# An attention-plus-FFN kernel on one core: inner passes row by row, a later divide, an earlier value projection and a later last norm

## The chip, the cores and the metric

The kernel runs on one NeuronCore of a Trainium2 chip. The metric is the device time of one execution in microseconds. Before the change the median of three runs is 858.41 us (858.38 to 859.41).

## The reference

The input x has 32 sequences of 256 tokens with 128 features. One layer of post-norm transformer is computed in float32:

```python
# attention: 16 heads of 8; scores get -(i - j) as a decay, and are causal
Q, K, V = (split_heads(x @ W.T + b) for W, b in ((Wq, bq), (Wk, bk), (Wv, bv)))
attn = softmax(where(j > i, -inf, Q @ K.T / sqrt(8)) - (i - j))
x = layernorm(x + (attn @ V) @ Wo.T + bo)
# FFN: every matrix is ternary times a power of two, with a scale per output
h = silu((x @ w1.T) * s1) * ((x @ w2.T) * s2)      # 128 -> 512
h = gelu((h @ h1.T) * sh1)                         # 512 -> 512
h = gelu((h @ h2.T) * sh2)                         # 512 -> 512
x = layernorm(x + (h @ w3.T) * s3)                 # 512 -> 128
```

## The kernel before

**Tiles and steps.** Sequences are handled in 16 pairs of 512 tokens. A step n of the function `step` has two stages. In the attention stage the scores of pair n are weighed (`weigh`) while the score maxima of pair n+1 are taken (`row_maxima`), in 12 iterations. In the feed stage the FFN of pair n-1 runs (`feed`), and the end of pair n's attention (`rest`) is woven between its parts. Nothing is planned by costs or due times: each engine works through its instructions in the order in which the program issues them, and that order is written out by hand with generators. A `yield` ends a piece; whoever holds the generator calls `next` where the following piece shall be issued. (The profile puts nearly every instruction on L56, because a helper there records them, so the tiles' names tell them apart.)

**Exact float32 out of two parts.** The FFN's activations are split into a rounded high part and a low part (`hi`, `lo`, the two slices of `h`, `hodd`, `heven`); each product with a weight block is two matmuls, one for each part. (The kernel tests at run time that the weights lose nothing in the rounded format, and takes this branch if so; the other branch isn't run here.) So each inner layer (h1 into `podd`, h2 into `peven`) has 4 output blocks o times 4 input blocks k times 2 parts, 32 matmuls of 128x512. Blocks o = 0 and 1 are accumulated together in one two-bank PSUM tile, then o = 2, then o = 3. In the first of these passes (line 586 on) the order before is: for o = 0 the blocks k = 0, 1, 2, for o = 1 the same, and then k = 3 for both. The gates write `h` block by block: ScalarE takes the silu (`sg`), VectorE multiplies (`h0w`), rounds it into the high part and subtracts for the low part; the low parts of blocks 0 and 1 are subtracted on GpSimd (line 576).

**What is woven in.** `feed` yields after each of its 4 gates, and ahead of each of the 8 outputs of the inner layers, 12 times in all. At each yield the next piece of `rest` is issued. Before the change those pieces are, in a step in the middle:

1. first half of the last `outputs` (`pa`);
2. its second half, and the copy `oT`;
3. the transposes `pt` and, on VectorE, the divide (`rec`, then `on` twice);
4. `maxima_to_rows` of pair n+1: transposes `pm`, high part `mhi` on ScalarE, low part `mlo` on VectorE, four DMAs on SP;
5. `finish`, first part: transposes `pon`, copy `onT`;
6. `project_values` of pair n+2: matmuls `pv`, four additions `vaug`;
7. `finish`, second part: matmuls `po`, residual addition into x;
8. `first_norm`, statistics `sta`, `mva`, `rsa` and a power on GpSimd (line 275);
9. its normalisation (`x<-x,mva,rsa`).

**The end of a pair.** `last` (pair n-2, in the attention stage of step n) has four pieces: the w3 matmuls `pw<-heven` with the scaling copy `yT`; transposes `py` and the residual `y`; the statistics `stf`, `mvf`, `rsf` with the power on GpSimd; and the normalisation `z` with the store of the result on SP's queue. They are issued in iterations 0, 2, 4 and 6. The heven that the first piece reads comes from the feed stage that has just ended.

**PSUM.** Six of the eight banks are three two-bank tiles (`two`) for scores, gates and inner layers; two banks (`work`) serve everything else, `pt`, `pm`, `pon`, `pv` and `po` among it, so each of those waits until the tile that held its bank has been read.

Of the kernel before, what the change touches and what calls it, by code (L numbers as in the profile page):

```python
# [17 lines left out]
P = 128  # L18
# [21 lines left out]
KC = HID // P  # L40
NPAIR = B // 2
# [18 lines left out]
def tile_attn_ffn(  # L60
# [24 lines left out]
    pe, vec, act, sp = (InOrder(tc, e) for e in (nc.tensor, nc.vector, nc.scalar, nc.sync))  # L85
# [24 lines left out]
    ks = [const.tile([P, W, TOK], F32R, name=f"ks{i}") for i in range(2)]  # L110
# [355 lines left out]
    def outputs(n, a):  # L466
        v = pairs[n]["v"]
        *first, second = pairs[n][("e", a)]
        r, e = divmod(a, 2)
        if e == 0:  # L470
            pairs[n]["pa"] = work(f"pa_{n}_{r}").rearrange("c (b i) -> c b i", b=2)
        pa = pairs[n]["pa"]
        for jc in range(2):
            for b in range(2):
                for c in range(C):
                    h, p = c // 2, c % 2
                    at = VSLOT * (C * r + c) + VHEAD * e
                    pe.matmul(
                        pa[32 * c : 32 * (c + 1), b, jc * P :],
                        lhsT=v[:, 2 * b + jc, at : at + 32],  # L480
                        rhs=second[:, p, h, b, :] if jc else first[h][:, p, b, :],
                        start=(e == b == jc == 0), stop=(e == b == jc == 1),
                        tile_position=(0, 32 * c),
                    )
            if jc == 0:
                yield
        if e == 0:
            return
        oT = op.tile([P, TOK], F32, name=f"oT_{n}_{r}", tag="oT", bufs=1)
        act.copy(oT, pa.rearrange("c b i -> c (b i)"))  # L490
        yield

        if r == 0:
            pairs[n]["on"] = op.tile([P, NT, D], F32, name=f"on_{n}", tag="on", bufs=1)
        on = pairs[n]["on"].rearrange("i t (r e c d) -> i t r e c d", r=2, e=2, c=C)
        po = work(f"pt_{n}_{r}").rearrange("i (t c k) -> i t c k", t=NT, c=C)
        for t in range(NT):
            pe.transpose(po[:, t].rearrange("i c k -> i (c k)"), oT[:, t * P : (t + 1) * P], ident)
        rec = mp.tile([P, NT, C, 2], F32, name=f"rec_{n}_{r}", tag="rec")
        vec.reciprocal(rec, po[:, :, :, HD : HD + VHEAD + 1 : VHEAD])  # L500
        for e in range(2):
            vec.tensor_tensor(
                on[:, :, r, e], po[:, :, :, VHEAD * e : VHEAD * e + HD],
                rec[:, :, :, e : e + 1].to_broadcast([P, NT, C, HD]), ALU.mult,
            )
# [40 lines left out]
    def product(ps, w, parts, start, stop):  # L546

        for i, part in enumerate(parts):
            pe.matmul(
                ps, lhsT=w, rhs=part, start=start and i == 0,  # L550
                stop=stop and i == len(parts) - 1,
            )

    def feed(n, exact, ws, hp, gp):

        final = n == NPAIR - 1
        even, odd = ("odd", "even") if final else ("even", "odd")
        x1T = pairs[n]["x1T"]
        parts = range(2 if exact else 1)
        kind = F32R if exact else F32  # L560
        h = hp.tile([P, len(parts), KC, TOK], kind, name=f"h0_{n}", tag=even)
        for o in range(KC):
            cols = slice(o * P, (o + 1) * P)
            pab = two(f"pw_{n}_{o}")
            pa, pb = pab[:, 0, :], pab[:, 1, :]
            product(pa, ws["w1"][:, 0, cols], [x1T[:, i, :] for i in parts], True, True)
            product(pb, ws["w2"][:, 0, cols], [x1T[:, i, :] for i in parts], True, True)
            sg = gp.tile([P, TOK], F32, name=f"sg_{n}_{o}", tag="sg")
            act.activation(sg, pa, AF.Silu, scale=sc["s1"][:, o : o + 1])
            whole = gp.tile([P, TOK], F32, name=f"h0w_{n}_{o}", tag="whole") if exact else h[:, 0, o, :]  # L570
            vec.scalar_tensor_tensor(
                whole, pb, sc["s2"][:, o : o + 1], sg, ALU.mult, ALU.mult
            )
            if exact:
                vec.tensor_copy(h[:, 0, o, :], whole)
                (nc.gpsimd if o < (1 if final else 2) else vec).tensor_tensor(  # L576
                    h[:, 1, o, :], whole, h[:, 0, o, :].bitcast(F32), ALU.subtract
                )
            yield
        prepare(AF.Gelu)  # L580
        for w, s, nm, tag in (
            (ws["h1"], sc["sh1"], "odd", odd), (ws["h2"], sc["sh2"], "even", even)
        ):
            got = hp.tile([P, len(parts), KC, TOK], kind, name=f"h{nm}_{n}", tag=tag)

            for os in ((0, 1), (2,), (3,)):
                both = two(f"p{nm}_{n}_{os[0]}")
                ph = {o: both[:, o - os[0], :] for o in os}
                for ks in ((0, 1, 2), (3,)):
                    for o in os:  # L590
                        for k in ks:
                            product(
                                ph[o], w[:, k, o * P : (o + 1) * P],
                                [h[:, i, k, :] for i in parts], k == 0, k == KC - 1,
                            )
                for o in os:
                    yield
                    if not exact:
                        act.activation(got[:, 0, o, :], ph[o], AF.Gelu, scale=s[:, o : o + 1])
                        continue  # L600
                    whole = gp.tile([P, TOK], F32, name=f"{nm}w_{n}_{o}", tag="whole")
                    hi, lo = (got[:, i, o, :] for i in range(2))
                    hasty = nm == "even" and o == KC - 1
                    if not hasty:
                        act.activation(hi, ph[o], AF.Gelu, scale=s[:, o : o + 1])
                    act.activation(whole, ph[o], AF.Gelu, scale=s[:, o : o + 1])
                    if hasty:
                        vec.tensor_copy(hi, whole)
                    vec.tensor_tensor(lo, whole, hi.bitcast(F32), ALU.subtract)
            h = got  # L610
        if n < NPAIR - 2:
            prepare(AF.Exp)
        elif not final:
            prepare(AF.Silu)
        pairs[n]["h"] = h
# [47 lines left out]
    def run(gen):  # L663
        for _ in gen:
            pass
# [25 lines left out]
    def step(n, exact=None, ws=None, hp=None, gp=None):  # L691


        side = iter(())
        settling = (
            last(n - 2, exact, ws, gp) if n > 1 else first_norm(0) if n else inexact_weights()
        )
        ahead = project(n + 2) if n + 2 < NPAIR else iter(())
        for i in range(3 * G):
            weigh(n, i)  # L700
            j = i if n else i + LEAD
            if n + 1 < NPAIR and j < 3 * G:
                row_maxima(n + 1, j)
            next(side, None)
            if n and i == 9:
                turn(n - 1, exact)
            if i in (0, 2, 4, 6) if n else i:
                next(settling, None)

            if i in ((3, 4, 5) if n == 1 else (1, 3, 5)):  # L710
                next(ahead, None)
            if i % 3 == 2:
                run(side)
                side = outputs(n, i // 3)
        run(settling)
        run(ahead)
        if n + 2 < NPAIR:
            stack(n + 2, "q")
            stack(n + 2, "k")


        def rest():
            yield from side
            yield
            if n + 1 < NPAIR:
                maxima_to_rows(n + 1)
                yield
            last_steps = finish(n)
            next(last_steps)
            yield  # L730
            if n + 2 < NPAIR:
                project_values(n + 2)
                yield
            yield from last_steps
            if n:
                yield
                yield from first_norm(n)
            if n == NPAIR - 1:
                yield
                turn(n, exact)  # L740

        if n:
            prepare(AF.Silu)
        due = rest()
        for _ in feed(n - 1, exact, ws, hp, gp) if n else ():
            next(due, None)
        run(due)
# [83 lines left out]
```

## Time and profile before

| what | value |
|---|---|
| median of 3 runs | 858.41 us |
| profiled execution, its own time | 859.17 us |
| its span | 857.4 us |
| PE busy | 799.5 us (93%) |
| weight loads (PEld) busy | 561.5 us (65%) |
| VectorE (DVE) busy | 635.0 us (74%) |
| ScalarE (ACT) busy | 519.5 us (61%) |
| GpSimd (POOL) busy | 270.9 us (32%) |
| one step in the middle (428.02 to 476.88) | 48.86 us, PE busy 48.02 |
| its attention stage (435.40 to 459.36) | 23.96 us, PE busy 23.37, DVE busy 21.11 |
| its gates and first inner layer (459.36 to 476.88) | 17.52 us, PE busy 17.27, DVE busy 13.50 |
| the next second inner layer (476.88 to 484.30) | 7.42 us, PE busy 7.42, DVE busy 3.83 |

The middle steps are equal: the second inner layers start 48.86 us apart from 134.87 to 721.18. The last three stretches of that kind are shorter (46.92, 45.68 and 43.62 us). Matmuls are pipelined, so a PE that is busy may still have started late: of two matmuls in a row, the distance of their starts tells more than their durations.

### The profile page before, as it was taken

Reading aid. Unit: us, or ns where it says so; the run is one execution under the profiler, and the core shown is the slowest. Engines: PE = TensorE matmul, PEld = TensorE weight load, DVE = VectorE, ACT = ScalarE, POOL = GpSimd, SP = SyncE. Lnnn points to the kernel's source line nnn. Section 1 sums busy time; section 2 is a strip of 40 time slices with the busy share of each in tenths; the row PEclk is TensorE's granted clock in tenths of the full one; section 3 lists DMA queues with packets and bytes.
Section 4 is the critical chain, followed back from the end, with each engine's and each line's share of the span. In section 5 each row is a group of like instructions: output and inputs, shape, how many; then the busy total and the mean of one; then the engine's idle time right before and its main releaser. Section 6 shows DMA issues by size and latency. Waiting matters only on the chain.

```text
span 857.4 us, 17396 instructions
## 1 busy us (share of the span) xinstructions
PE 799.5 (93%) x7042; PEld 561.5 (65%) x7042; DVE 635.0 (74%) x1231; ACT 519.5 (61%) x713; POOL 270.9 (32%) x354
## 2 busy tenths in 40 slices
PE   4588999999999999999999999999999999999895
PEld 2355667676766767676766767676676767666673
DVE  3677677878778686878778787878778687874664
ACT  1026367666576676657676666657666666658462
POOL 9123332414232241414233240524224141424200
PEclk9558699999999999999999999999999999999998
DMA  6543240220405041140404032040504013000001
GB/s 142 128 147 86 45 101 16 61 67 14 102 14 114 14 101 26 38 90 14 103 13 112 16 74 54 14 102 14 115 13 111 5 48 68 14 5 13 1 1 29
DMA packets 40627, 48.16 MB, mean 56 GB/s; under 512 B 4376, under 2 KB 22040, under 8 KB 40536
## 3 DMA queue, kind: packets, MB, share of 16 engines
q1 hardware_dynamic: 38240, 44.13, 21.8%
q10 hardware_dynamic: 2296, 2.82, 1.4%
q8 instruction: 57, 0.93, 0.5%
q14 instruction: 34, 0.28, 0.1%
HBM read 7.48 MB, written 4.19 MB: 14 GB/s over the span
## 4 chain that ended last, share of the span: by engine, by line
PE 63%; DVE 24%; ACT 5%; issue 3%; DMA 2%; POOL 2%; ACTq 0%; DVEq 0%; POOLq 0%
PE peven L56 13%; PE s L56 9%; PE podd L56 9%; DVE m L56 9%; PE pw L56 8%; PE pa L56 8%; DVE h L56 5%; DVE h0w L56 3%; PE s_0d L56 2%; DVE z L56 2%; PE s_3d L56 2%; PE po L56 2%; PE pq L56 2%; PE pv L56 2%; ACT sg L56 1%
## 5 line engine op out<-in xcount | busy, mean ns | idle before, releaser
L459 POOL TENSOR_SCALAR_AFFINE_SELECT e<-e 128x512 f32<-128x512 f32 x128 | 82.5, 644 | 275.2 <-ACT e L56 275.2
L56 DVE TENSOR_REDUCE m<-s 128x4 f32<-128x1024 f32 x128 | 155.5, 1218 | 16.3 <-PE s L56 16.1
L56 ACT ACTIVATE e<-s 128x1024 f32<-128x1024 f32 x128 | 130.9, 1022 | 55.8 <-PE s L56 26.9
L56 PE MATMUL podd<-h,h_near 128*128 128x512 f32 x512 | 142.8, 414 | 3.8 <-DVE h L56 3.4
L56 PE MATMUL peven<-hodd,h_near 128*128 128x512 f32 x512 | 122.1, 395 | 0.0
L56 PEld LDWEIGHTS podd<-h,h_near 128*128 128x128 f32 x512 | 91.7, 190 | 37.1 <-DVE h L56 20.8
L56 PEld LDWEIGHTS peven<-hodd,h_near 128*128 128x128 f32 x512 | 95.9, 188 | 23.4
L56 ACT ACTIVATE hodd<-podd,sh 128x512 fp32r<-128x512 f32 x64 | 44.1, 689 | 76.3 <-PE podd L56 76.3
L56 DVE TENSOR_TENSOR heven<-evenw,heven 128x512 fp32r<-128x512 f32 x64 | 44.3, 693 | 48.0 <-ACT evenw L56 47.5
L56 PE MATMUL pw<-x1T,w_near 128*128 128x512 f32 x256 | 75.5, 418 | 0.9 <-DVE h0w L56 0.9
L56 PEld LDWEIGHTS s<-qs,ks 64*128 64x128 f32 x512 | 39.9, 191 | 55.3 <-issue 28.4
L56 PE MATMUL s<-qs,ks 64*128 64x256 f32 x512 | 67.0, 339 | 6.5 <-DVE m L56 6.4
L56 PE MATMUL pa<-e,vaug 128*32 128x256 f32 x1024 | 71.5, 393 | 0.1
L56 DVE SCALAR_TENSOR_TENSOR h0w<-pw,s,sg 128x512 f32<-128x512 f32 x64 | 47.9, 748 | 30.1 <-ACT sg L56 30.1
L275 POOL TENSOR_TENSOR rsa<-rsa,half 128x4 f32<-128x4 f32 x16 | 16.5, 1033 | 169.6 <-DVE rsa L56 169.5
L56 ACT ACT_TABLE_LOAD x47 | 60.3, 1283 | 3.4 <-issue 2.6
L56 PE MATMUL s<-ks,qs 62*128 62x256 f32 x512 | 59.1, 309 | 2.7 <-DVE m L56 1.4
L56 ACT ACTIVATE sg<-pw,s 128x512 f32<-128x512 f32 x64 | 43.8, 685 | 28.1 <-PE pw L56 27.7
L56 ACT ACTIVATE heven<-peven,sh 128x512 fp32r<-128x512 f32 x48 | 33.4, 696 | 39.0 <-PE peven L56 39.0
L576 POOL TENSOR_TENSOR h<-h0w,h 128x512 fp32r<-128x512 f32 x31 | 40.0, 1290 | 52.6 <-DVE h L56 52.6
L56 PEld LDWEIGHTS pw<-x1T,w_near 128*128 128x128 f32 x256 | 43.4, 188 | 18.1 <-ACT nothing L56 5.8
L56 DVE TENSOR_TENSOR hodd<-oddw,hodd 128x512 fp32r<-128x512 f32 x64 | 44.0, 688 | 13.9 <-ACT oddw L56 13.7
(145 smaller groups left out, 1425.8 us busy)
## 6 DMA issues: line engine op xcount, KB each, us to landing
qs<-qhi SPq DMA_DIRECT2D x32, 256.0 KB
qs<-qlo SPq DMA_DIRECT2D x32, 256.0 KB
ks<-khi SPq DMA_DIRECT2D x28, 256.0 KB
ks<-klo SPq DMA_DIRECT2D x28, 256.0 KB
x<-in_x_dram SPq DMA_DIRECT2D x16, 256.0 KB
out_dram<-z SPq DMA_DIRECT2D x16, 256.0 KB
ks<-khi ACTq DMA_DIRECT2D x4, 256.0 KB
ks<-klo ACTq DMA_DIRECT2D x4, 256.0 KB
```

Source lines behind the costliest of these rows:

```text
L56: return lambda *args, **kw: self.tc.keep_in_program_order(call(*args, **kw))
L275: nc.gpsimd.tensor_tensor(rs, rs, half, ALU.pow)
L459: nc.gpsimd.affine_select(out=on_diagonal, in_=on_diagonal, pattern=[[0, on_diagonal.shape[1]], [1, P]], base=0, channel_multiplier=-1, co ...
L576: (nc.gpsimd if o < (1 if final else 2) else vec).tensor_tensor(h[:, 1, o, :], whole, h[:, 0, o, :].bitcast(F32), ALU.subtract)
```

## The change

In `outputs` a `yield` is put between the transposes `pt` and the divide. In `rest` the first three pieces are taken one by one, and the divide is issued behind `maxima_to_rows`, in the same piece. `project_values` moves ahead of `finish`, whose two parts become pieces 6 and 7. From step 2 on, the last two pieces of `last` are no longer issued in iterations 4 and 6 of the attention stage, but at the end of `rest`, as pieces 10 and 11: the statistics ahead of the second output of the h2 layer, the normalisation and its store ahead of the third. In `feed` the first pass of an inner layer goes through k and the two parts outside, and through o = 0 and 1 inside; passes over a single o keep their order.

```diff
@@ outputs
             pe.transpose(po[:, t].rearrange("i c k -> i (c k)"), oT[:, t * P : (t + 1) * P], ident)
+        yield
         rec = mp.tile([P, NT, C, 2], F32, name=f"rec_{n}_{r}", tag="rec")
@@ feed
-                for ks in ((0, 1, 2), (3,)):
-                    for o in os:
-                        for k in ks:
-                            product(
-                                ph[o], w[:, k, o * P : (o + 1) * P],
-                                [h[:, i, k, :] for i in parts], k == 0, k == KC - 1,
+                for k in range(KC):
+                    for i in parts:
+                        for o in os:
+                            pe.matmul(
+                                ph[o], lhsT=w[:, k, o * P : (o + 1) * P], rhs=h[:, i, k, :],
+                                start=k == i == 0, stop=k == KC - 1 and i == parts[-1],
                             )
@@ step
-            if i in (0, 2, 4, 6) if n else i:
+            if i in ((0, 2) if n > 1 else (0, 2, 4, 6)) if n else i:
                 next(settling, None)
...
-        run(settling)
+        if n < 2:
+            run(settling)
         run(ahead)
@@ rest
-            yield from side
-            yield
+            for _ in range(3):
+                next(side)
+                yield
             if n + 1 < NPAIR:
                 maxima_to_rows(n + 1)
+            run(side)
+            yield
+            if n + 2 < NPAIR:
+                project_values(n + 2)
                 yield
             last_steps = finish(n)
             next(last_steps)
             yield
-            if n + 2 < NPAIR:
-                project_values(n + 2)
-                yield
             yield from last_steps
...
                 turn(n, exact)
+            if n > 1:
+                yield
+                yield from settling
```

## The prediction

> **What bounds the kernel now.** First the busy row of the page: PE is busy for 93% of the span and no other engine for more than 74%. That doesn't say where it starts late, so next the stretches of one middle step, by stage: attention, gates with the first inner layer, second inner layer (columns: length, then busy time of PE, weight loads, DVE, ACT, POOL, then granted clock, DMA share, GB/s).
>
> ```profile
> PE 799.5 (93%) x7042; PEld 561.5 (65%) x7042; DVE 635.0 (74%) x1231; ACT 519.5 (61%) x713; POOL 270.9 (32%) x354
> ...
> 435.40:459.36 23.96, 23.37 (x301) 15.66 (x300) 21.11 (x35) 16.50 (x20) 10.94 (x16) 1.00 0.05 13
> 459.36:476.88 17.52, 17.27 (x113) 12.61 (x110) 13.50 (x28) 10.90 (x17) 3.67 (x3) 1.00 0.56 124
> 476.88:484.30 7.42, 7.42 (x34) 5.68 (x33) 3.83 (x15) 4.85 (x8) 1.01 (x1) 1.00 0.13 35
> ```
>
> The reader is to see that attention loads DVE almost as much as PE, and the second inner layer leaves DVE half idle. Then the chain that ended last, within that step (start, us, what): from 465.24 to 469.97 it is DVE alone, gate 2, the divide, gate 3, and only then PE.
>
> ```profile
> 465.24 0.76 DVE h0w L56
> ...
> 466.58 0.69 DVE h L56
> ...
> 467.28 0.28 DVE rec L56
> ...
> 467.79 0.28 DVE on L56
> 468.07 0.67 DVE h0w L56
> ...
> 469.22 0.70 DVE h L56
> ...
> 469.97 0.97 PE podd L56 x3
> ```
>
> Last, PE's timeline, where the bracket is the idle time before a group and its releaser: one wait in attention, one in the first inner pass. In the latter the start distances show more than the bracket does: 16 matmuls from 465.96 to `pon` at 470.77 take 4.81 us, though eight undisturbed ones take 1.87 (the chain), 0.233 each, so that 16 need 0.32 (first distance) + 15 x 0.233 = 3.82.
>
> ```profile
> 454.12 0.51 PE L56 MATMUL s<-qs,ks 64*128 64x256 f32 x4 [0.51 <-DVE m L56]
> ...
> 465.96 3.78 PE L56 MATMUL podd<-h,h_near 128*128 128x512 f32 x13
> 469.97 0.97 PE L56 MATMUL podd<-h,h_near 128*128 128x512 f32 x3 [0.23 <-DVE h L56]
> 470.77 0.60 PE L56 MATMUL pon<-ident,on 128*128 128x128 f32 x4
> ```
>
> So a middle step loses 0.99 us at the gates and 0.58 in attention (`pt` at 452.96 needs 0.58, so the next could start at 453.54, not 454.12). Everything below is in the clock of this step.
>
> **Divide and row order.** Both work on the 0.99. Without the divide between, h0w of gate 3 starts at 467.19 instead of 467.98, and all that follows is 0.79 earlier: high part of block 3 ready at 468.40, low part at 469.12. The low part of block 2 stays at 467.27. In the new order the 16 matmuls are k0, k1, k2, k3, each high, high, low, low; number p starts at 465.96 + 0.32 + (p-2) x 0.233. Block 2's high part is wanted by number 9 at 467.91 (there since 466.55), its low by 11 at 468.38, block 3's high by 13 at 468.84, its low by 15 at 469.31. No wait is left; the slot behind the sixteenth is 469.78. Of the two parts the divide is worth most (row order alone still waits for the low part until 469.96: 0.2 gained). ACT isn't hurt: before, `hodd` starts at 470.98, behind the sixteenth matmul and not the fourteenth, so that o = 0 ending later costs nothing.
>
> Unknown is whether alternating the two banks slows matmuls. The nearest row is `pw`, two matmuls in one bank, two in the other: starts 0.230 apart in a bank, 0.235 across. By it 32 alternations a step cost at most 0.16. **A rule speaks against the change:** the Trainium skill, "TensorE: Matmul & The Clock Gate", section "A second HAM failure mode: psum-queue depth-cycling", says that 512-column matmuls that cycle through PSUM banks left small gaps in which the clock fell to half again and again. The trace has the half clock elsewhere (transposes 0.213 apart near 85 us, 0.109 here). One throttled stretch of 3.4 us a step would cost 1.7 us, 22 us over 13 steps. But the pairs of score matmuls alternate banks as well, and the granted clock of all three stretches is 1.00. I take 0, keep 0.16 for the range, and make the rule a rival.
>
> **Value projection first.** `pv` now stands behind `podd`. As built it takes the bank that `pm` had, so it waits for `mlo`: DVE 468.43 (last subtraction) + 0.61 = 469.04, + 0.67 = 469.71, just ahead of the slot at 469.78. `pv` takes 0.89, to 470.67; `pon` needs the divide, now behind `mlo`: 469.64 + 0.38 + 0.21 + 0.28 = 470.51, in time. `pon` 0.44, so the second pass starts at 471.11, with some 0.05 for a restart at 471.16, instead of 472.02: **0.86 gained**. Had `pv` to wait for the divide, 0.78 of it would go; that is the bound. Queued on DVE behind: `vaug` 470.93 to 471.73, low part of hodd 0 to 472.34, `onT` to 473.03; `po` wants it at 471.16 + 1.94 = 473.10. That is covered by 0.07 only. `pm`'s four DMAs keep their place on SP.
>
> **Last norm among the inner layers.** Attention sheds four `stf` (0.77 by start distances), four `mvf` (0.40), `rsf` (0.08), four `z` (1.39), 2.64 us of DVE, and a POOL power (1.02) from between its masks. But PE waits for DVE only at 454.12, so **0.58** is all that this gives: PE was busy in 23.37 of 23.96. The store moves on SP from ahead of the 8 score-row DMAs to behind the `mhi`/`mlo` ones; behind it stands only the next x load, needed a step later.
>
> The work lands where DVE is half idle, but at the end, between the low parts that the w3 matmuls of the next stage read at once:
>
> ```profile
> 481.95 0.69 DVE L56 TENSOR_TENSOR heven<-evenw,heven 128x512 fp32r<-128x512 f32 x1 [2.02 <-ACT evenw L56]
> ...
> 485.56 0.69 DVE L56 TENSOR_TENSOR heven<-evenw,heven 128x512 fp32r<-128x512 f32 x1
> ...
> 850.00 0.17 DVE L56 TENSOR_SCALAR rsf<-mvf 128x4 f32<-128x4 f32 x1
> 851.30 1.11 DVE L56 TENSOR_SCALAR z<-y,mvf,rsf 128x128 f32<-128x128 f32 x4 [1.12 <-POOL rsf L275]
> ```
>
> From low part 0 at 481.95: + 0.61; statistics 1.27 (838.63 to 839.81, + 0.08), low part 1 from 483.83 to 484.44. `rsf` starts at 483.74, and by the pair of rows at 850 `z` can start 1.30 later, at 485.04: DVE idles 0.6. `z` takes 1.02 (842.37 to 843.39, POOL idle), low part 2 0.61, rounding of block 3 0.46, low part 3 0.69: ready at **487.82** instead of 486.25. Eight w3 matmuls start from 485.12 on, the last, which reads it, at 486.85; now 487.87. **1.03 lost a step**, 0.4 if `z` needn't wait for POOL, 1.4 if its third piece takes 0.70 as it does in attention.
>
> **The sum.** Steps 1 to 13, gates: 13 x -0.86 = -11.2. Attention of step 2, whose feed before had no deferred norm: -0.58. Of 3 to 13: 11 x (1.03 - 0.58) = +4.95. Of 14 (its wait for DVE is only 0.43): +0.6. Feed of step 14, without `pv` to cover the divide: -0.2.
> Step 15: before, `pon` stands ahead of the first pass and PE idles for it, and the pass then runs at a lowered clock:
>
> ```profile
> 801.41 0.63 PE L56 MATMUL pon<-ident,on 128*128 128x128 f32 x4 [3.08 <-DVE on L56]
> 801.79 5.51 PE L56 MATMUL podd<-h,h_near 128*128 128x512 f32 x16
> ```
>
> After, with neither maxima nor values, `pon` falls behind the pass, which starts near 798.2, is held by gate 3 (low part at 802.37) and ends at 802.94 instead of 807.14. `po` then waits for `onT` until 804.55, `turn` moves behind the even pass, and ACT ends its gelus 3.3 us earlier; the norm holds up DVE before the last gates by 0.8, the last pass gains 0.2: **-2.7** (-1 to -4).
> Step 0 has no feed to hide anything, and half the clock. `pv` starts at 87.39 as before, now `pon` (0.85) and `onT` stand behind it and `vaug`: `onT` to 91.1, `po` 1.71, to 92.85 instead of 90.97: **+1.9**.
> Together -7.2: span 857.4 to 850.2. The profiled execution took 859.17, 1.8 outside its span, and the median is 858.41, so **851.2**.
>
> **Rivals.** (A) The w3 stall doesn't appear, because DVE or POOL are quicker there, as the last step of before suggests, where a norm among the inner layers delays one w3 matmul by 0.23: 12 x 1.03 come back, **839**. Against it: only `z` stands ahead of low part 1 there, the statistics are earlier. (B) `pv` waits for the divide, or `onT` misses `po`: 0.78 a step lost, 13 x 0.78 = +10: **861**. For it: margins of 0.07. Against: the bank is `pm`'s. (C) Slower: bank alternation in the first passes. It decides from 7.2 / (13 x 32) = 17 ns a matmul; at one throttled window a step, **873**. Against: 5 ns in `pw`.
>
> **How the numbers follow.** Likeliest 0.64, own range 846 to 855 (z's bounds: 12 x -0.6, 12 x +0.37; step 15's). A 0.15, B 0.10, C 0.11. The range leaves out about a tenth at each end: 840 to 860. A difference within 0.2% (1.7 us) is about what a measurement of this kernel can't tell from none. Faster: the likeliest, A and a few of B, 0.81; same 0.05; slower 0.14.
>
> **What would show it.** In the profile after: `podd` x16 of a middle step from first start to `pv` 3.8 us, without a wait for `h`; `pv` at once behind it; no wait for DVE near the ninth score group; a wait of about 1 us of `pw<-heven` for `heven`; stages of about 24.4 and 24.0 us, 48.4 together. Start distances above 0.245 in a first pass, or a clock under 1.00, are C. `pv` waiting for `on` is B. Wrong would also be made by a first layer that no longer hides `onT`, or a step 0 that re-times the clock.

## The result, and the profile after

The changed kernel takes **856.34 us** (median of 14 runs, 854.21 to 857.15), the kernel before, run beside it on the same chip, 857.98 us (14 runs, 856.17 to 860.17). The ratio is 0.9975, interval 0.9965 to 0.9984: faster, but by a quarter of a per cent. The forecast was 851.2, or 0.8% faster. The time lies within the forecast's range of 840 to 860, but outside the likeliest case's own range of 846 to 855: the sign was right and the size wrong.

The two profiled executions took 859.17 us before (span 857.4) and 855.48 after (span 853.7). That pair differs by 3.7 us and the medians by 1.6, because the profiled run of before was 1.2 over its median and that of after 0.9 under. The accounting below is made between the two profiles.

First the busy row of the page of after:

```profile
PE 795.8 (93%) x7042; PEld 559.3 (66%) x7042; DVE 628.6 (74%) x1231; ACT 520.3 (61%) x713; POOL 277.9 (33%) x354
```

PE is busy for 3.7 us less than before (799.5), the whole difference of the spans; its idle time is 57.9 us both times, and only its places have changed. Next the same three stages of a middle step as in the prediction, after the change: gates with the first inner layer, second inner layer, attention (columns: length, busy time of PE, weight loads, DVE, ACT, POOL, granted clock, DMA share, GB/s).

```profile
458.95:475.52 16.57, 16.57 (x112) 12.44 (x109) 13.22 (x27) 10.87 (x17) 3.67 (x3) 1.00 0.61 132
475.52:483.05 7.53, 7.53 (x33) 5.81 (x31) 4.84 (x24) 4.84 (x8) 1.25 (x2) 1.00 0.00 0
483.05:507.70 24.65, 23.79 (x301) 15.59 (x300) 20.09 (x27) 16.57 (x20) 11.33 (x16) 1.00 0.09 24
```

The gates stage has no idle PE left (16.57 busy of 16.57, before 17.27 of 17.52), and DVE does about a microsecond more in the second inner layer and less in attention. But the attention stage, which should have become shorter by 0.58 and longer by 1.03, is 24.65 us instead of 23.96, and PE now idles in it for 0.86 us, where it idled for 0.59. The step is 48.75 us after 48.86.

The chain that ended last shows both halves of it, first the gates, then the end of the second inner layer (start, us, what).

```profile
465.78 3.73 PE podd L56 x16
469.51 0.99 PE pv L56 x8
470.50 0.44 PE pon L56 x4
470.94 1.87 PE podd L56 x8
472.81 1.02 PE po L56 x8
...
480.77 0.69 DVE heven L56
481.46 0.78 DVE stf L56 x4
482.25 0.29 DVE mvf L56 x4
...
482.56 0.18 DVE rsf L56
...
482.81 1.39 POOL rsf L275
...
484.23 1.12 DVE z L56 x4
485.35 0.95 DVE heven L56 x2
...
486.32 0.70 DVE heven L56
...
487.07 0.49 PE pw L56
```

Where gate 2, the divide and gate 3 stood before, there is now PE without a break: `podd`, `pv`, `pon`, `podd`, `po`. In exchange the chain runs for 6.24 us, from low part 0 at 480.77 to the end of low part 3 at 487.01, over DVE and GpSimd, and what waits for it are the last products of w3, twice. PE's timeline of the same place, with the ninth score group of the attention stage that follows:

```profile
465.53 3.98 PE L56 MATMUL podd<-h,h_near 128*128 128x512 f32 x16
469.35 1.15 PE L56 MATMUL pv<-wv_sb,xT 128*128 128x128 f32 x8
...
483.95 1.42 PE L56 MATMUL pw<-heven,w_near 128*128 128x512 f32 x5
486.00 0.83 PE L56 MATMUL pw<-heven,w_near 128*128 128x512 f32 x2 [0.63 <-DVE heven L56]
487.07 0.49 PE L56 MATMUL pw<-heven,w_near 128*128 128x512 f32 x1 [0.23 <-DVE heven L56]
487.49 0.50 PE L56 MATMUL s<-qs,ks 64*128 64x256 f32 x4
...
502.59 0.50 PE L56 MATMUL s<-qs,ks 64*128 64x256 f32 x4
```

Sixteen `podd` take 3.82 us from 465.53 to `pv`, exactly as forecast; the wait of 0.51 in front of the ninth score group is gone. The w3 products take 3.54 us from their first start to the next scores (483.95 to 487.49), against 2.05 before: **1.49 us lost a step, where 1.03 was forecast.**

The sum, by the starts of the feed's first product (`pw<-x1T`) in each step of the two profiles:

| stretch | forecast | measured |
|---|---|---|
| start to step 1's feed | +1.9 | 117.36 to 119.09: +1.73 |
| step 1's feed to step 2's | -1.44 | 48.88 to 47.38: -1.50 |
| eleven middle steps (step 2's to 13's) | -4.5 | 537.44 to 536.28: -1.16 |
| step 13's to 14's | -0.26 | +0.05 |
| step 14's to 15's | -0.2 | 41.48 to 41.21: -0.27 |
| step 15's feed to the end | -2.7 | 65.5 to 63.0: -2.5 |
| all | -7.2 | -3.7 |

Start and end came out within 0.2 us each, as sums. The miss sits in the middle steps: 3.3 of 3.5 us.

### The profile page after: what moved, and what is told of

It reads as the page before. It is cut to its first block, busy times and chain, and to the rows that moved or that the text cites. A ratio compares the mean times of both kernels' runs of the same rounds, so it can differ in the third digit from the quotient of the medians.

```text
span 853.7 us, 17421 instructions
## 1 busy us (share of the span) xinstructions
PE 795.8 (93%) x7042; PEld 559.3 (66%) x7042; DVE 628.6 (74%) x1231; ACT 520.3 (61%) x713; POOL 277.9 (33%) x354
## 4 chain that ended last, share of the span: by engine, by line
PE 76%; DVE 11%; ACT 5%; POOL 4%; issue 2%; DMA 1%; ACTq 0%; POOLq 0%; DVEq 0%
PE podd L56 13%; PE pa L56 11%; PE s L56 11%; PE peven L56 8%; PE pw L56 8%; DVE heven L56 4%; PE s_0d L56 2%; POOL rsf L275 2%; PE s_2d L56 2%; PE s_3d L56 2%; PE s_1d L56 2%; PE po L56 2%; PE pt L56 2%; DVE z L56 2%; PE pq L56 2%
## 5 line engine op out<-in xcount | busy, mean ns | idle before, releaser
L56 ACT ACTIVATE e<-s 128x1024 f32<-128x1024 f32 x128 | 130.6, 1020 | 49.9 <-PE s L56 32.4
L459 POOL TENSOR_SCALAR_AFFINE_SELECT e<-e 128x512 f32<-128x512 f32 x128 | 84.4, 659 | 209.9 <-ACT e L56 209.9
L56 PE MATMUL podd<-h,h_near 128*128 128x512 f32 x512 | 131.3, 403 | 0.4 <-DVE h L56 0.4
L275 POOL TENSOR_TENSOR rsf<-rsf,half 128x4 f32<-128x4 f32 x16 | 21.0, 1313 | 97.2 <-DVE rsf L56 97.2
```

The source lines that it names most:

```text
L56: return lambda *args, **kw: self.tc.keep_in_program_order(call(*args, **kw))
L275: nc.gpsimd.tensor_tensor(rs, rs, half, ALU.pow)
L459: nc.gpsimd.affine_select(out=on_diagonal, in_=on_diagonal, pattern=[[0, on_diagonal.shape[1]], [1, P]], base=0, channel_multiplier=-1, co ...
```

## The experiments

The reading to be tested: the miss is one term, the place of the last norm. It takes back nearly all that the gates give, and it costs more than forecast because GpSimd's power takes 1.38 us there instead of 1.02. Against it stand the readings that the gates give less than their part of the sum, and that the power is slower for another reason than its neighbour on DVE. Every kernel below computes all of the reference.

**1. The change without the late norm** (`no_late_norm`), against the kernel after:

```diff
-            if i in ((0, 2) if n > 1 else (0, 2, 4, 6)) if n else i:
+            if i in (0, 2, 4, 6) if n else i:
...
-        if n < 2:
-            run(settling)
+        run(settling)
...
-            if n > 1:
-                yield
-                yield from settling
```

> The changed kernel with the last norm back in iterations 4 and 6 of attention; divide, values and row order stay. My theory: the 0.75 us a step that the gates gained is kept, the wait of pw<-heven for heven (1.49 us) is gone, the wait for DVE near the ninth score group (with what goes with it, 0.85 us) is back. Middle step 48.11 us, w3 matmuls of a middle step 2.05 us from first start to the next scores, ratio to the kernel before about 0.986 (846 us). Rival, that the late norm costs nothing and the gates gained little: step about 48.75, ratio 0.997.

847.52 us (846.88 to 848.26), ratio to before 0.9878 (0.9863 to 0.9893); the middle step is 48.10. PE's timeline:

```profile
481.68 2.11 PE L56 MATMUL pw<-heven,w_near 128*128 128x512 f32 x8
483.72 0.50 PE L56 MATMUL s<-qs,ks 64*128 64x256 f32 x4
```

Without the late norm the eight w3 products run in one piece again, 2.04 us to the next scores, and the rest of the change is worth 0.76 a step and 10 us in all. So the gates part did give nearly what the sum said; the late norm alone takes 0.65 a step back.

**2. The late norm alone** (`only_late_norm`): the kernel before with the last two hunks of the diff in `step` and `rest`.

```diff
-            if i in (0, 2, 4, 6) if n else i:
+            if i in ((0, 2) if n > 1 else (0, 2, 4, 6)) if n else i:
...
-        run(settling)
+        if n < 2:
+            run(settling)
...
+            if n > 1:
+                yield
+                yield from settling
```

> The kernel before with nothing but the last norm moved behind the first norm, in pieces 10 and 11. My theory: each middle step gains 0.85 us in attention and loses 1.49 us at the w3 matmuls, so 49.50 us instead of 48.86; 11 such steps, some 1 us more in the last two: about 866 us, ratio 1.009. Rival: attention's relief is what made the changed kernel faster; then the step is under 48.86 and the ratio under 1.

867.22 us (864.41 to 868.61), ratio 1.0099 (1.0085 to 1.0113); step 49.51, that is +0.65.

```profile
490.46 1.42 PE L56 MATMUL pw<-heven,w_near 128*128 128x512 f32 x5
492.52 0.84 PE L56 MATMUL pw<-heven,w_near 128*128 128x512 f32 x2 [0.64 <-DVE heven L56]
493.58 0.50 PE L56 MATMUL pw<-heven,w_near 128*128 128x512 f32 x1 [0.22 <-DVE heven L56]
```

The same two waits stand there without any of the other edits. The parts add up: -0.76 and +0.65 make the -0.11 of the whole. The late norm is a loss by itself, 1% of the time.

**3. The last norm beside the first one** (`norm_beside_first`), against the kernel after. The work still leaves the attention stage, but is issued with the pieces of `first_norm`, ahead of the second inner layer's outputs and no longer between its low parts:

```diff
-                yield from first_norm(n)
+                for _ in first_norm(n):
+                    if n > 1:
+                        next(settling)
+                    yield
+            if n > 1:
+                run(settling)
...
-            if n > 1:
-                yield
-                yield from settling
```

> The changed kernel with the late norm two pieces earlier: its statistics behind those of the first norm (piece 8), its normalisation behind the first norm's (piece 9), where DVE stands idle until the second inner layer's first outputs. My theory: both gains stay and neither wait comes: step 48.86 - 0.75 - 0.85 = 47.26 us, in all about 22 us less than before, 836 us, ratio 0.974. Rival: any place in the feed stage makes a low part late; then pw<-heven or peven<-hodd wait by 0.5 us or more a step, and the ratio stays above 0.985.

838.63 us (837.93 to 840.32), ratio 0.9773 (0.9759 to 0.9786); step 47.40. The timeline of DVE, POOL and PE:

```profile
470.77 0.17 DVE L56 TENSOR_SCALAR rsf<-mvf 128x4 f32<-128x4 f32 x1
471.01 1.39 POOL L275 TENSOR_TENSOR rsf<-rsf,half 128x4 f32<-128x4 f32 x1 [0.23 <-DVE rsf L56]
472.47 1.11 DVE L56 TENSOR_SCALAR z<-y,mvf,rsf 128x128 f32<-128x128 f32 x4
474.02 0.69 DVE L56 TENSOR_TENSOR heven<-evenw,heven 128x512 fp32r<-128x512 f32 x1 [0.44 <-ACT evenw L56]
...
477.20 2.11 PE L56 MATMUL pw<-heven,w_near 128*128 128x512 f32 x8
479.24 0.50 PE L56 MATMUL s<-qs,ks 64*128 64x256 f32 x4
```

`z` is done 0.44 us before low part 0 of `heven` starts, and the w3 products don't wait. The power takes 1.39 here too, and it costs nothing. So what hurts is not the length of the power but what stands behind it in DVE's order. The step is 0.70 shorter than in experiment 1: that is what taking the norm out of attention brings where nothing is paid for it. It is 0.14 longer than expected.

**4. The norm in one piece** (`norm_in_one_piece`, a single run), against the kernel after. The power then has no subtraction beside it, at the price of all of the norm standing ahead of low part 1:

```diff
             if n > 1:
                 yield
-                yield from settling
+                run(settling)
```

> The changed kernel with the late norm's statistics and normalisation in one piece, so that no subtraction with two SBUF inputs runs on DVE while GpSimd raises rsf to its power; DVE waits for it instead. Theory: the power took 1.38 us in the changed kernel because the subtraction of heven's second low part started just before it; here it takes 1.02, and the last low part is ready some 0.2 us later than in the changed kernel. Rival: the power is slow there for another reason, and takes 1.38 again, the last low part then 0.6 later.

892.81 us, against 857.82 for before: much slower. First POOL and ACT in one step of its timeline:

```profile
295.45 1.01 POOL L275 TENSOR_TENSOR rsf<-rsf,half 128x4 f32<-128x4 f32 x1 [5.28 <-DVE rsf L56]
...
298.31 0.69 ACT L56 ACTIVATE evenw<-peven,sh 128x512 f32<-128x512 f32 x1 [2.61 <-DVE heven L56]
```

Then PE's timeline around the w3 products of another step:

```profile
346.45 0.96 PE L56 MATMUL pw<-heven,w_near 128*128 128x512 f32 x3
348.13 1.74 PE L56 MATMUL pw<-heven,w_near 128*128 128x512 f32 x4 [0.72 <-DVE heven L56]
350.10 0.50 PE L56 MATMUL pw<-heven,w_near 128*128 128x512 f32 x1 [0.23 <-DVE heven L56]
```

And three windows (columns as above): the stretch that these waits fall into, what follows it, and the same place one step later:

```profile
347.22:350.64 3.42, 2.33 (x8) 0.97 (x9) 3.17 (x6) 2.44 (x4) 0.00 (x0) 1.00 0.55 151
350.64:360.88 10.24, 10.16 (x69) 6.46 (x70) 5.41 (x6) 4.19 (x5) 4.67 (x8) 0.50 0.01 2
401.84:405.25 3.41, 2.53 (x9) 1.15 (x9) 3.09 (x5) 3.05 (x5) 0.00 (x0) 1.00 0.55 154
```

The disputed number is settled: the power takes 1.01 us when no subtraction has begun ahead of it. But the expected time failed twice. The last low part comes 6.77 us after low part 0 begins, later by 0.53 than in the kernel after and not by 0.2: one of `evenw`'s buffers comes free only behind low part 1, so ACT waits 2.61 us before the last block's `evenw`. And behind these waits, in every third of the middle steps, the granted clock is 0.50 for 10.2 us; those steps last 53.9 to 54.1 us, the others 49.9. This kernel is no measure of the power's price in time.

**5. The row order alone** (`rows_only`): before with only the hunk in `feed`.

```diff
-                for ks in ((0, 1, 2), (3,)):
-                    for o in os:
-                        for k in ks:
-                            product(
...
+                for k in range(KC):
+                    for i in parts:
+                        for o in os:
+                            pe.matmul(
```

> The kernel before with nothing but the row order of the first inner passes. My theory: block 3's low part still comes at its old time behind the divide, so the sixteen matmuls take about 4.57 us from first start to pon instead of 4.81; 0.24 a step gained, ratio about 0.996. Rival, that alternating PSUM banks cost time or clock: start distances of the sixteen above 0.235 where nothing is waited for, or a granted clock under 1.00 in the middle, and a ratio above 1.

855.07 us (853.04 to 856.99), ratio 0.9969 (0.9958 to 0.998); step 48.63, so -0.23.

```profile
462.55 3.03 PE L56 MATMUL podd<-h,h_near 128*128 128x512 f32 x12
465.85 1.46 PE L56 MATMUL podd<-h,h_near 128*128 128x512 f32 x4 [0.27 <-DVE h L56]
467.15 0.60 PE L56 MATMUL pon<-ident,on 128*128 128x128 f32 x4
```

With the divide still between the gates the pass waits for a part of `h` and takes 4.60 us, 0.21 less than before, as the prediction worked out (0.2). Starts lie 0.23 apart and the clock is 1.00 from 92.7 to 795.9 us: alternating the banks costs nothing that can be seen.

**6. The old passes, everything else of experiment 1** (`old_passes`):

```diff
-                for k in range(KC):
-                    for i in parts:
-                        for o in os:
...
+                for ks in ((0, 1, 2), (3,)):
+                    for o in os:
+                        for k in ks:
```

> The kernel with the late norm back in attention (ratio 0.988 to the kernel before), and the old order of the first inner passes as well: what is left of the change is the divide behind the last gate and the values first. My theory: only the wait for block 2's low part stays (0.2 us), less 0.1 because pv then needn't wait for mlo; step about 48.2, ratio about 0.9895. Rival, that the row order carries the gain: step near 48.8, ratio 0.998 or more.

848.15 us (847.8 to 848.62), ratio 0.9885 (0.9866 to 0.9903); step 48.21. The intervals of 1 and 6 overlap, but their steps differ by 0.11: sixteen `podd` take 4.07 us from 462.23 to `pv` instead of 3.82. Divide and values are worth 0.65 a step, the row order 0.11 on top of them, 0.23 without them.

**7. The values behind `pon` again, everything else of experiment 1** (`values_behind`):

```diff
             run(side)
             yield
-            if n + 2 < NPAIR:
-                project_values(n + 2)
-                yield
             last_steps = finish(n)
             next(last_steps)
             yield
+            if n + 2 < NPAIR:
+                project_values(n + 2)
+                yield
```

> The kernel with the late norm back in attention (ratio 0.988 to the kernel before), and the value projection again behind the first part of finish: what is left is the divide behind the last gate and the row order. My theory: pon then stands right behind the sixteen matmuls and waits for the divide, 0.78 us; the gates gain only 0.2, step about 48.65, ratio about 0.996. Rival, that the divide's place alone makes the gain and the order of pv and pon is free: step 48.1, ratio 0.988.

852.86 us (852.28 to 853.21), ratio 0.9938 (0.9922 to 0.9954); step 48.78, so only 0.08 better than before, and less than the 0.23 of the row order alone.

```profile
464.00 3.98 PE L56 MATMUL podd<-h,h_near 128*128 128x512 f32 x16
468.71 0.63 PE L56 MATMUL pon<-ident,on 128*128 128x128 f32 x4 [0.74 <-DVE on L56]
```

`podd` has its 3.82, and then `pon` stands 0.9 us behind the free slot at 467.82, waiting for the later divide. The order of `pv` and `pon` is therefore not free: without the values ahead, the divide behind the last gate costs more than it gives (48.78 against the 48.63 of the row order alone). This is the 0.78 that the prediction named as the price of a lost cover, measured at 0.68 a step (48.78 less 48.10). The values ahead with the divide left between the gates was not run.

**8. Experiment 3 with step 0 as before** (`norm_beside_first_old_start`):

```diff
         def rest():
+            if not n:
+                run(side)
+                maxima_to_rows(n + 1)
+                last_steps = finish(n)
+                next(last_steps)
+                project_values(n + 2)
+                run(last_steps)
+                return
```

> The kernel with the late norm beside the first norm (ratio 0.977 to the kernel before), with the order of before in step 0 alone, which has no feed stage to hide anything. My theory: po of step 0 no longer waits for onT behind vaug, 1.6 us less, ratio about 0.9755. Rival: step 0 hides its order behind the load of the flag and the waits for the clock; no difference to 0.977.

837.31 us (834.73 to 838.79), ratio 0.9755 (0.9735 to 0.9775): faster than both kernels. It isn't secured as better than experiment 3, whose interval overlaps. In the profiles step 1's feed starts at 117.03 instead of 120.41, but 1.35 of these 3.38 us lie ahead of step 0's `pt`, where the two kernels have the same order.

## Why the prediction was wrong in size

**Gates: right, slightly over.** Forecast 0.86, measured 0.75 (first feed product to the start of the second inner layer, 17.33 to 16.58). The step to 3.82 us for sixteen `podd` held to the hundredth, with the divide out of the way as its larger part (experiments 5 and 6). Up to the second pass the gain is 0.89 (it starts 12.63 us behind the feed's first product before and 11.74 after). The rest went at `po`, whose weight load waits for `onT`:

```profile
472.68 0.97 PEld L56 LDWEIGHTS po<-wo_sb,onT 128*128 128x128 f32 x8 [0.30 <-DVE onT L56]
```

From start to start the eight `podd` ahead of it take 1.98 us instead of 1.93, and `po` 0.91 instead of 0.81. The margin of 0.07 that the prediction gave `onT` was too small, and these 0.15 are its price.

**Attention: under.** Forecast 0.58, measured 0.85, from the scores behind w3 to the next feed (21.08 to 20.23). The wait at the ninth score group gave 0.57 of it, as forecast: from `pt` to those scores it is 1.16 us before and 0.59 after. Behind that group another 0.12 is gained, where `px1T` starts 1.00 us behind `pa` instead of 1.15; the prediction had no term for it. The last 0.15 belongs to the stall: the first score group, right behind the last w3 product, takes 0.67 us where it took 0.82. Experiment 3, which has no stall, lacks these 0.15, and over experiment 1 it puts the relief alone at 0.70.

**The w3 stall: the step that failed.** The mechanism is as forecast; its size is 1.49 and not 1.03. Of the 0.46, 0.36 are one row: the prediction took for the power the pair of rows at 850 us, 1.02 and `z` 1.30 behind `rsf`. In the middle steps it is this (DVE and POOL of after):

```profile
482.56 0.17 DVE L56 TENSOR_SCALAR rsf<-mvf 128x4 f32<-128x4 f32 x1
482.64 0.69 DVE L56 TENSOR_TENSOR heven<-evenw,heven 128x512 fp32r<-128x512 f32 x1
482.81 1.38 POOL L275 TENSOR_TENSOR rsf<-rsf,half 128x4 f32<-128x4 f32 x1 [5.29 <-DVE rsf L56]
484.23 1.12 DVE L56 TENSOR_SCALAR z<-y,mvf,rsf 128x128 f32<-128x128 f32 x4 [0.91 <-POOL rsf L275]
```

The rest, 0.10, is a restart behind the last single product (487.07 to 487.49, 0.42 where the forecast had the next scores one slot later). No run has the short power at this place with all else equal, so that its 0.36 makes as much of the stall is read from the chain, in which `z` waits for it.

DVE subtracts low part 1 beside the power and began 0.17 us ahead of it. In the ten profiles of this study all 56 powers of which that is true take 1.38 or 1.39 us, and all 264 others 1.01 to 1.03, 119 of them with a subtraction that begins 0.53 us behind the power's start. Not every work of DVE does this: in 103 of the 264, DVE had begun a maximum or statistics, with one input each, 0.17 to 0.18 us before. The trace of before held the answer: its timeline has a power behind a subtraction too, at 810.87 us, and it takes 1.38.

```profile
810.70 0.69 DVE L56 TENSOR_TENSOR hodd<-oddw,hodd 128x512 fp32r<-128x512 f32 x1
810.87 1.38 POOL L275 TENSOR_TENSOR rsa<-rsa,half 128x4 f32<-128x4 f32 x1 [11.40 <-DVE rsa L56]
```

The Trainium skill, "SBUF — State Buffer", section "SBUF: two separate sides", says that a DVE operation with two inputs in SBUF and a GpSimd operation that reads SBUF exclude each other: whichever starts first holds the port for its whole length. In the first order the traces agree in direction: the subtraction ends 0.52 us behind the power's start, and the power ends 0.37 us later than alone. In the other order a power held to its end would keep the subtraction waiting for some 0.5 us; it takes 0.69 us like all others, so no run here shows that the power holds it up. The choice of the row should have been made by what runs beside it, not by the tile's name.

The stall of the forecast, put right by these two terms, is 1.03 + 0.36 + 0.10 = 1.49. Of the 0.46 a step that this is over the forecast, the larger relief in attention gave 0.27 back and the smaller gain at the gates took another 0.11: 0.30 a step, 3.3 us in eleven steps. These are the profiled runs, 3.7 us apart; that the medians are only 1.6 apart is 2.1 us more of a miss, for which no row of the traces stands (the last section has what the runs show of it).

**Steps 0 and 15: right in sum.** In step 0 the new order costs 2.00 us where 1.9 was forecast: from the first `pt` to the last `po` starts it is 6.71 us before and 8.71 after, and 8.71 or 8.72 in the other four kernels with this order. The 1.73 of the table comes near by luck: ahead of `pt` the profile of after is 0.69 later and behind `po` 0.96 shorter, and such differences come without the order too. `only_late_norm`, whose step 0 is that of before, reaches step 1's feed at 119.53, later than after. In step 15 PE doesn't idle ahead of `podd` (797.03 and not 801.79), and the half clock that the prediction showed there is gone; up to the last feed it gained 3.75, and then the last norm held the gates up by more than forecast:

```profile
816.48 1.38 POOL L275 TENSOR_TENSOR rsf<-rsf,half 128x4 f32<-128x4 f32 x1 [8.09 <-DVE rsf L56]
...
821.39 1.20 PE L56 MATMUL pw<-x1T,w_near 128*128 128x512 f32 x4 [2.25 <-DVE h0w L56]
```

The first w3 product comes 6.24 us behind the last feed's start, where it was 4.86: 1.38 lost instead of 0.8, with the long power once more in it.

**The rivals.** A (no stall) fell: the stall is there in every middle step and larger. B (`pv` waits for the divide, or `onT` misses `po`) fell in size: `pv` doesn't wait for the divide, and the miss of `onT` costs 0.15 a step and not 0.78; experiment 7 shows what it costs when the order isn't as built. C (bank alternation, clock) fell: starts 0.229 to 0.235 apart behind the first, clock 1.00 in all three stages, and a gain in experiment 5, so the small gaps of the rule that the prediction cites don't appear here. What was wrong in the weighing is the range of the likeliest case. It took +0.37 a step for the stall, where the stall itself missed by 0.46, and its 846 to 855 is narrower than the bounds that it names: z's alone, 12 x -0.6 and 12 x +0.37, reach from 844.0 to 855.6.

## What to carry to other kernels

Before work is moved to where an engine is half idle, ask what stands behind it in that engine's own order and who reads that next: the same norm costs 0.65 us a step between the low parts that the next products wait for and brings 0.70 a few outputs earlier. A chain that hops from DVE to GpSimd and back is priced by the row whose neighbours on both engines are the same, because the same tiny power took 1.02 or 1.38 us by what DVE had begun 0.17 us before. And a part of a change that only pays with another (the divide with the values, 0.65 together; with the row order, but without the values, 0.08) is to be costed as a pair.

## What else the runs showed

**Half clock from short waits.** In experiment 4 waits of 0.72, 0.14 and 0.23 us (the second is hidden within a row of the timeline) came ahead of 10.2 us at half clock, in some steps and not in others. The traces tell which. In all ten profiles the changes of the granted clock lie whole multiples of 3.413 us apart: 802.52 and 805.93 in before, or 350.64 and 360.88 in experiment 4, which is three of them. Three steps of experiment 4 take 153.7 to 153.8 us, and 45 of these stretches 153.6, so in every third step the waits fall at the same place of a stretch. In four steps all three waits lie in one stretch, to within 0.04 us (from 193.62, 347.22, 500.82 and 654.42); PE is busy for 2.32 to 2.37 us of it, and at its end the clock falls. In the steps between they are spread over two stretches, PE is busy for at least 2.52 us of each, and the clock holds, except once (at 763.65). In the kernel after, with waits of 0.63 and 0.23 us, no stretch of the middle steps has less than 2.55, and the clock is 1.00 from 104.0 to 844.7. So the waits and where they fall go with the half clock; that they cause it is inferred. It is no limit for all work: in after the stretch from 817.39 has 1.75 us of busy PE and the clock holds.

**The start sets a part of the spread.** A stretch at half clock begins in step 0 at 81 to 84 us in the profiles and ends at 102.8 in before, 104.0 in after and 92.7 in `rows_only`; in `norm_beside_first_old_start` it is 83.9 to 90.7 and 94.1 to 100.9. The mean granted clock of each run goes with its time. Of the 19 runs of before beside experiment 5, the 12 with 0.957 to 0.962 take 856.54 to 858.04 us and the 7 with 0.953 to 0.956 take 858.38 to 860.29. Of the 14 runs of after, the 4 with 0.957 to 0.960 take 854.21 to 854.75 and the 10 with 0.952 to 0.955 take 855.41 to 857.15. At like clocks the medians are 2.3 and 2.7 us apart, so a part of what lies between the 1.6 us of the medians and the 3.7 of the profiles is likely the start. Whether the change itself makes the lower clock more frequent wasn't tried. The spread of the runs of one kernel (before: 856.17 to 860.17) is larger than the gain that this change was measured at.
